# A recurrent layer with its input product in seven half products per chunk of 16 steps

## Chip, cores and metric

The kernel runs on one core of one Trainium2 chip. The metric is the device time of one execution in microseconds. The engines are named as in the profile: PE is TensorE, DVE is VectorE, ACT is ScalarE, POOL is GpSimd, SP is SyncE, which here only issues DMAs.

## What is computed

```python
def reference(x, cond, Wx, Wh, b, W1, b1, W2, b2):     # x: (64, 256, 1024), cond: (64, 1024), all f32
    # layer 0: a recurrence over the 256 steps, and a residual
    xW = einsum('ntd,dh->nth', x, Wx) + b
    h = cond
    for t in range(256):
        h = tanh(h @ Wh + xW[:, t])
        x[:, t] = x[:, t] + h
    # layer 1: a Haar transform along time, every coefficient times one gate, and back, and a residual
    g = silu(cond @ W1.T + b1)
    gate = sigmoid(g @ W2.T + b2)
    return x + haar_back(gate * haar(x))               # = x * (1 + gate) up to rounding, for the gate is one per (n, d)
```

The kernel before and the kernel after both use that the gate doesn't depend on time: each step's x + h is multiplied by a factor made once from the gate. What remains is the recurrence (64 x 1024 by 1024 x 1024, 256 times in sequence) and the product of x with Wx (16384 x 1024 by 1024 x 1024), which depends on nothing but the inputs.

## The kernel before

**The recurrent product.** `h_product` (L208) multiplies the hidden state (64 x 1024, in four quadrants of 32 rows by half the columns) with Wh by seven products of halves (Strassen's scheme in Winograd's form): four sums of quadrants of h are made by DVE in `strassen_sides` (L190), the sums of Wh were made once in `strassen_weight` (L141). Each of the seven is 4 x 4 matmuls of f32 on a quarter of the array's columns (`strassen_product`, L158; the profile shows two matmuls for each). Some results accumulate in the PSUM bank `acc`, into which `put` (L202) has copied the step's row of x Wx beforehand, others in the banks `m16` and `m57`; DVE adds them to y (L222, L225) and h (L229), ACT takes the tanh (L393), DVE transposes h in blocks of 32 x 32 to hT (L395). hT is what the next step's product needs.

**The input product.** `XWork` (L245) does x Wx for a pair of steps, 128 rows at once. DVE splits x into a part of few mantissa bits (`high_bits`, L116), the rest (L253) and a mixture of both (L255), each of them in the reduced f32 form[...]; Wx was split the same way at the start and stays in SBUF. Three products, low, high and mixed, give the full precision. The stationary operand is a block of x (128 x 128), the moving one a half row block of Wx (128 x 512): 8 x 3 x 2 = 48 matmuls of 128x512 for two steps (L237), into the banks `main` and `mixed`. ACT takes `mixed` out (L269), POOL adds the bias (L270), DVE adds `main` (L301). The sum goes to DRAM and comes back as rows for each step (L305, L311).

**The output.** For each step POOL adds hT to x (L416) and multiplies by the factor (L372); SP stores a pair of steps. The first pairs, which are ready ahead of the factor, are kept in DRAM and scaled later.

**What sets the order.** The source gives an order, in which `first` and `second` spread the 48 matmuls of a later pair over two steps, behind the recurrent product of each. The tile framework then plans the order on each engine's queue from expected durations: an instruction that is expected to be ready may go ahead of an earlier one of the source. [...]

## Time and profile before

| | |
|---|---|
| median of 3 runs | 3133.39 us (3131.64 to 3136.84) |
| profiled execution, its own time | 3132.18 us |
| profiled execution, span of the trace | 3130.4 us |
| mean granted clock of PE | 0.997 |
| PE busy | 3090.0 us, 99% |
| DVE busy | 1762.4 us, 56% |
| POOL busy | 1112.9 us, 36% |
| ACT busy | 717.9 us, 23% |
| DMA | 298.54 MB, mean 95 GB/s |

The groups of the page give a mean duration per instruction. For PE it is the time from a matmul's start to its modelled end, and matmuls are pipelined, so the cost of one is read from the timeline as the distance of starts. A duration on DVE or POOL includes the time in which the instruction was held after it had started.

### The profile page before, as it was taken

The numbers are of one execution on the slowest core, as the hardware profiler recorded it, in microseconds if no ns is written. First come the engines' busy times: TensorE is split into PE (matmuls) and PEld (weight loads), VectorE is DVE, ScalarE is ACT, GpSimd is POOL, SyncE is SP. The second block draws the span as 40 slices with busy tenths as digits, with TensorE's granted clock in tenths as the row PEclk, the third lists the DMA queues.
The fourth block names the chain that finished last, engine by engine and source line by source line (L and its number), as shares of the span: only waits on it lengthen the run. The fifth ranks groups of instructions, "written<-read, shape, count | busy, mean of one in ns | idle before, by whom it ended". The sixth has DMA issues, their size and how long they took to land.

```text
span 3130.4 us, 137359 instructions
## 1 busy us (share of the span) xinstructions
PE 3090.0 (99%) x63648; PEld 2696.5 (86%) x63648; DVE 1762.4 (56%) x2736; ACT 717.9 (23%) x1425; POOL 1112.9 (36%) x768
## 2 busy tenths in 40 slices
PE   7999999999999999999999999999999999999998
PEld 4888888888888888888888888888888888888887
DVE  6455555555555555555555555555555555555564
ACT  3222222222222222222222222222222222222221
POOL 0233433333333334333333433333333333333332
PEclk9999999999999999999999999999999999999999
DMA  6332332222222222222222222222222222222222
GB/s 241 114 103 97 103 103 90 93 87 96 89 90 91 89 91 91 92 89 91 92 90 90 92 94 86 93 90 90 91 89 97 85 93 93 90 91 89 91 76 70
DMA packets 146286, 298.54 MB, mean 95 GB/s; under 512 B 25520, under 2 KB 91568, under 8 KB 145712
## 3 DMA queue, kind: packets, MB, share of 16 engines
q1 hardware_dynamic: 142448, 283.99, 26.8%
q8 instruction: 498, 8.16, 1.1%
q10 hardware_dynamic: 3264, 5.77, 0.5%
q14 instruction: 76, 0.62, 0.1%
HBM read 153.88 MB, written 135.79 MB: 93 GB/s over the span
## 4 chain that ended last, share of the span: by engine, by line
PE 97%; DMA 1%; DVE 1%; issue 0%; ACT 0%; SPq 0%; POOL 0%; ACTq 0%; DVEq 0%
PE main L237 30%; PE m L163 29%; PE acc L163 21%; PE mixed L237 16%; DMA w<-w1T 1%; PE gate_ps L180 1%; DMA xw<-sum_d 0%; DVE h L229 0%; DMA h0T<-condT 0%; ACT h L393 0%; DVE hT L395 0%; DVE s L195 0%; DVE s L193 0%; DVE s L194 0%; PE acc L180 0%
## 5 line engine op out<-in xcount | busy, mean ns | idle before, releaser
L416 POOL TENSOR_TENSOR x<-x,hT 128x512 f32<-128x512 f32 x254 | 448.9, 1767 | 1684.2 <-DVE hT L395 1673.3
L237 PE MATMUL main<-wx,x 128*128 128x512 f32 x4096 | 993.0, 394 | 4.9 <-DVE sum L301 2.9
L237 PEld LDWEIGHTS main<-wx,x 128*128 128x128 f32 x4096 | 759.5, 188 | 188.5 <-issue 27.7
L222 DVE TENSOR_TENSOR y<-m,u 128x256 f32<-128x256 f32 x255 | 108.2, 424 | 865.6 <-PE m L163 865.6
L237 PE MATMUL mixed<-wx,x 128*128 128x512 f32 x2048 | 505.6, 398 | 0.0
L163 PE MATMUL m<-t,s 128*32 128x128 f32 x16320 | 494.2, 273 | 2.4 <-DVE s L195 2.4
L237 PEld LDWEIGHTS mixed<-wx,x 128*128 128x128 f32 x2048 | 376.1, 188 | 100.5 <-issue 25.0
L163 PEld LDWEIGHTS m<-t,s 128*32 128x32 f32 x16320 | 452.4, 110 | 3.0 <-issue 2.9
L270 POOL TENSOR_TENSOR sum<-sum,b_row 128x512 f32<-128x512 f32 x256 | 328.8, 1285 | 281.0 <-ACT sum L269 281.0
L393 ACT ACTIVATE h<-h 128x512 f32<-128x512 f32 x256 | 161.9, 633 | 794.7 <-DVE h L229 794.7
L372 POOL TENSOR_TENSOR x<-x,factor 128x512 f32<-128x512 f32 x248 | 336.6, 1358 | 11.5 <-DVE factor L358 1.8
L229 DVE TENSOR_TENSOR h<-acc,y 128x512 f32<-128x512 f32 x255 | 176.4, 692 | 243.5 <-PE acc L163 243.5
L395 DVE STREAM_TRANSPOSE hT<-h 128x512 f32<-128x512 f32 x256 | 182.3, 712 | 204.0 <-ACT h L393 204.0
L163 PEld LDWEIGHTS m<-wh,hT 128*32 128x32 f32 x8160 | 208.1, 109 | 93.1 <-issue 84.9
L255 DVE SCALAR_TENSOR_TENSOR x<-x,x_high 128x1024 fp32r<-128x1024 f32 x128 | 287.7, 2248 | 0.0
L163 PE MATMUL m<-wh,hT 128*32 128x128 f32 x8160 | 276.0, 276 | 4.6 <-DVE hT L395 4.6
L163 PE MATMUL acc<-wh,s 128*32 128x128 f32 x8160 | 272.6, 273 | 2.9 <-issue 2.9
L163 PE MATMUL acc<-t,hT 128*32 128x128 f32 x8160 | 270.5, 273 | 2.1 <-issue 2.1
L163 PE MATMUL acc<-wh,hT 128*32 128x128 f32 x8160 | 271.4, 274 | 1.0 <-ACT acc L205 0.9
L163 PE MATMUL m<-wh,s 128*32 128x128 f32 x8160 | 269.9, 273 | 0.0
L261 ACT CAST x<-x_high 128x1024 fp32r<-128x1024 f32 x128 | 134.0, 1047 | 472.6 <-PE main L237 471.0
L163 PEld LDWEIGHTS acc<-wh,s 128*32 128x32 f32 x8160 | 229.6, 110 | 4.4 <-issue 4.4
(48 smaller groups left out, 2297.5 us busy)
## 6 DMA issues: line engine op xcount, KB each, us to landing
x<-xT SPq DMA_DIRECT2D x128, 512.0 KB, 3.7
sum_d<-sum SPq DMA_DIRECT2D x128, 512.0 KB, 3.0
xw<-sum_d SPq DMA_DIRECT2D x1024, 64.0 KB, 2.0
yT<-x SPq DMA_DIRECT2D x124, 512.0 KB, 3.6
wh<-wh ACTq DMA_DIRECT2D x8, 512.0 KB, 6.6
wx<-wx SPq DMA_DIRECT2D x8, 512.0 KB, 5.8
w<-w1T SPq DMA_DIRECT2D x8, 512.0 KB, 6.9
w<-w2T SPq DMA_DIRECT2D x8, 512.0 KB, 4.0
```

Source lines behind the costliest of these rows:

```text
L163: nc.tensor.matmul(out=out[q * R : (q + 1) * R], lhsT=a[:, k * R : (k + 1) * R], rhs=wh_s[i][k][:, q], start=first and k == 0, stop=k == K ...
L180: nc.tensor.matmul(out=ps[q * R : (q + 1) * R, g * F : (g + 1) * F], lhsT=vT[:, col : col + R], rhs=w[:, q * F : (q + 1) * F], start=k == ...
L222: nc.vector.tensor_add(y[:, 1:3], m57[:, : 2 * E].rearrange("p (i e) -> p i e", i=2), u[:].unsqueeze(1).broadcast_to((P, 2, E)))
L229: nc.vector.tensor_add(h, acc, flat(y))
L237: nc.tensor.matmul(out=acc[h], lhsT=v[:, k * P : (k + 1) * P], rhs=wx_s[k][which][:, h * HALF : (h + 1) * HALF], start=start and k == 0, s ...
L255: nc.vector.scalar_tensor_tensor(out=self.x2, in0=self.x1[:].bitcast(F32), scalar=-UP, in1=self.high, op0=ALU.mult, op1=ALU.add)
L261: nc.scalar.copy(self.x0, self.high)
L270: nc.gpsimd.tensor_add(s, s, b_row[:, h * HALF : (h + 1) * HALF])
L372: nc.gpsimd.tensor_mul(of_step(x, s), of_step(x, s), blocks(factor))
L393: nc.scalar.activation(h, h, AF.Tanh)
L395: nc.vector.transpose(hT, h)
L416: nc.gpsimd.tensor_add(of_step(x, s), of_step(x, s), blocks(hT))
```

## The change

The product of x with Wx is now made for chunks. The first eight steps are two chunks of 4 steps, as are the last eight; between them are 15 chunks of 16 steps.

- **Operands.** Blocks of Wx are stationary, x is the moving operand; the result has the columns of Wx on the partitions, so that the bias is one value for each partition and is added by ACT on its way out.
- **A chunk of 16 steps** is a matrix of two halves of 8 steps (512 rows of x each) by two halves of d; it is multiplied with Wx by seven products of halves in the same scheme as the recurrent product. POOL makes the four sums of x and the sums of results; DVE splits seven operands of two tiles each; where a result is a sum of two products, ACT puts the earlier one into the PSUM bank beforehand.
- **Forms.** The three split forms of the blocks of Wx and of their four sums (seven of the eight are used in a long chunk) are stored in DRAM at the start and in the first four steps, and are streamed to SBUF for each column block, in three buffers of 128 x 1536.
- **Rows.** Results go to DRAM and come back as 64 x 1024 for each step, not yet transposed; `put` is a transpose by DVE from SBUF into the PSUM bank, in place of ACT's copy.
- **Output.** x for the output is loaded for each step apart, in the layout of hT, and stored for each step.
- **Pace.** `due` gives deadlines: five products of a chunk by the step ahead of it, seven by its eighth step; each step of the recurrence does as much x work as the steepest of them asks for.
- The recurrent product has the same matmuls; its quadrants are ordered otherwise.

The core of the diff (removed: `XWork`, `load_x` for pairs, ACT's copy in `put`):

```diff
-        nc.scalar.copy(acc, flat(xw))
+        nc.vector.transpose(acc, flat(v))
...
+    def split_x(x, name: str) -> list:
+        x0 = high_bits(x[:], 2 * HALF, f"high_{name}")
+        out = [split.tile([P, 2 * HALF], F32R, tag=f"x{i}", bufs=(3, 4, 4)[i], name=f"x{i}_{name}") for i in range(3)]
+        nc.vector.tensor_sub(out[1], x, x0)
+        nc.scalar.copy(out[0], x0)
+        nc.vector.scalar_tensor_tensor(
+            out=out[2], in0=out[1][:].bitcast(F32), scalar=-UP, in1=x0, op0=ALU.mult, op1=ALU.add
+        )
+        return out
...
+    def x_banks(name: str) -> list:
+        return [x_pool.tile([P, HALF], F32, tag=tag, name=f"{tag}_{name}") for tag in ("mixed", "main")]
+
+    def take(out, mixed, main, b=0.0) -> None:
+        nc.scalar.activation(out, mixed, AF.Identity if b is not 0.0 else AF.Copy, scale=-DOWN, bias=b)
+        nc.vector.scalar_tensor_tensor(out=out, in0=main, scalar=1.0 + DOWN, in1=out, op0=ALU.mult, op1=ALU.add)
...
+    def load_forms(i: int, j: int, name: str):
+        w = stream.tile([P, KB, FORMS, P], F32R, tag="stream", name=name)
+        nc.sync.dma_start(out=w[:].bitcast(F32).rearrange("p k i f -> p k (i f)"), in_=forms_d[i][j])
+        return w
+
+    def products(banks, w, x, width: int, first: bool, last: bool, onto: bool = False):
+        mixed, main = banks
+        per = 2 * HALF // width
+        for form, out in ((2, mixed), (1, main), (0, main)):
+            for k in range(KB):
+                begins = first and k == 0 and (form == 1 or (form == 2 and not onto))
+                x_matmul(
+                    out, w[:, k, form], x[k // per][form], k % per, form,
+                    begins, last and k == KB - 1 and form != 1, width,
+                )
+            if form or not last:
+                yield width
...
+    def long_chunk(t: int):
...
+        order = ("M1", "M5", "M6", "M3", "M2", "M7", "M4")
+        ready = prepare(order[0])
+        for n, p in enumerate(order):
+            x, i = ready, int(p[1]) - 1
+            base = {"M6": m1, "M3": m5, "M2": m1, "M4": u}.get(p)
+            for j in range(KB):
+                w = load_forms(i, j, f"w{t}_{i}{j}")
+                if j == 0 and n + 1 < len(order):
+                    ready = prepare(order[n + 1])
+                mixed, main = x_banks(f"{t}_{i}{j}")
+                if base:
+                    nc.scalar.activation(mixed, base[j], AF.Copy, scale=-UP)
+                yield from products((mixed, main), w, x, HALF, True, True, onto=base is not None)
...
+                elif p == "M6":
+                    u[j] = part("u", j)
+                    take(u[j], mixed, main)
+                    nc.gpsimd.tensor_add(m5[j], m5[j], u[j])
+                elif p == "M7":
...
+                    take(m7, mixed, main)
+                    nc.gpsimd.tensor_add(results[p][:, :, j], by_rows(m5[j][:]), by_rows(m7[:]))
+                    nc.gpsimd.tensor_add(u[j], u[j], m7)
...
+                if j == KB - 1 and p in ("M3", "M2", "M7", "M4"):
+                    keep_result(results[p], t if p in ("M3", "M2") else half2, BLOCK, int(p in ("M3", "M7")))
+                yield HALF
...
     for t in range(T):
...
+            acc = put(xw_next, t + 1)
+        for _ in range(4):
+            next(weight_sums, None)
+        goal = done + max(((d - done) / max(by - t, 1) for d, by in deadlines if d > done), default=0)
+        while done < goal:
+            done += KB * next(work_x)
+        if t + 1 < T:
+            x_next = load_step(t + 1)
+        if t + 2 < T:
+            xw_next = xw_step(t + 2)
+
+        nc.gpsimd.tensor_add(x, x, hT)
...
+            nc.gpsimd.tensor_mul(x, x, factor)
+            nc.sync.dma_start(out=yT[t], in_=x)
```

## The prediction

> **What bounds the kernel now.** I read first the busy shares, then the chain that ended last, then the groups of its lines.

> ```profile
> PE 3090.0 (99%) x63648; PEld 2696.5 (86%) x63648; DVE 1762.4 (56%) x2736; ACT 717.9 (23%) x1425; POOL 1112.9 (36%) x768
> ...
> PE 97%; DMA 1%; DVE 1%; issue 0%; ACT 0%; SPq 0%; POOL 0%; ACTq 0%; DVEq 0%
> ...
> L237 PE MATMUL main<-wx,x 128*128 128x512 f32 x4096 | 993.0, 394 | 4.9 <-DVE sum L301 2.9
> ...
> L255 DVE SCALAR_TENSOR_TENSOR x<-x,x_high 128x1024 fp32r<-128x1024 f32 x128 | 287.7, 2248 | 0.0
> ```

> PE is busy 99% and is 97% of the chain, so PE work is the time. The timeline of 1505 to 1530 us gives its price: a block of 24 x products (128x512) starts at 1517.38 and the next recurrent product at 1523.04, so one costs 5.66/24 = 0.236 us; a recurrent product takes 6.26 us (1511.12 to 1517.38). A step is 6.26 + 5.66 = 11.92 us. What could replace PE shows in the same timeline, where VectorE and GpSimd hold each other up:

> ```profile
> 1507.80 0.29 DVE L193 TENSOR_TENSOR s<-hT 128x128 f32<-128x128 f32 x1
> 1507.84 1.39 POOL L416 TENSOR_TENSOR x<-x,hT 128x512 f32<-128x512 f32 x1 [8.17 <-DVE hT L395]
> 1508.00 1.38 DVE L194 TENSOR_TENSOR s<-hT 128x128 f32<-128x128 f32 x1
> ...
> 1519.67 1.18 DVE L253 TENSOR_TENSOR x<-x,x_high 128x1024 fp32r<-128x1024 f32 x1
> 1519.82 2.17 POOL L416 TENSOR_TENSOR x<-x,hT 128x512 f32<-128x512 f32 x1 [4.35 <-DVE hT L395]
> ```

> L194 needs 0.29 us but takes 1.38, until the GpSimd add ends; at 1519.82 the add waits for L253 instead. These rows also show the order: L253 of a later pair runs between hT and the sides of this step, so each queue was ordered by a planner that fills expected gaps, not by the source. I therefore do not count every source-order wait as a stall.

> The waits and the stretches give the slack and the DMA rate:

> ```profile
> DVE h L229 <- PE acc L163: 243.5, 255, 2.7
> DVE hT L395 <- ACT h L393: 204.0, 255, 1.2
> ...
> SPq L441 <- POOL x L372: 431.1, 124, 4.8
> ...
> 0.00:40.00 40.00, 26.23 (x228) 11.09 (x231) 28.14 (x34) 13.77 (x13) 0.20 (x4) 1.00 0.88 326
> ...
> 1500.00:2900.00 1400.00, 1400.00 (x29222) 1232.00 (x29215) 788.49 (x1235) 320.25 (x647) 512.78 (x352) 1.00 0.27 91
> ```

> VectorE rests about 0.95 us per step before h and 0.80 before hT (244/255, 204/255). DMA stands at 0.27 in the steady part; at the start it reached 326 GB/s at a share of 0.88. Last, a rest of PE costs more than itself:

> ```profile
> 1511.12 1.08 PE L163 MATMUL m<-wh,hT 128*32 128x128 f32 x32
> ...
> 3104.90 1.33 PE L163 MATMUL m<-wh,hT 128*32 128x128 f32 x32 [2.25 <-DVE hT L395]
> 3105.98 1.95 PE L163 MATMUL acc<-wh,hT 128*32 128x128 f32 x32
> ```

> After 2.25 us of rest the second block of 32 takes 1.95 us where it takes 1.06 in the steady part.

> [...]

> **The change part by part.**

> PE: out go 6144 x products of 512 columns (1450 us). In come 15 chunks of 7 x 4 x 4 x 3 = 336, that is 5040 x 0.236 = 1189 us, and four short chunks of 192 with 256 columns, 768. A 256-column product isn't in the trace: 0.118 (half) if columns set it, 0.188 if the weight load does; I take 0.15, 115 us (91 to 144). **Saved: 146 us (117 to 170)**. A step of a long chunk needs 6.26 + 21 x 0.236 = 11.22 us. The recurrent products keep shape and number.

> VectorE, uncontended, per 16 steps. Kept: h 0.69, hT 0.71, four sides at 0.29, y 0.42 and 0.29. Added: the transpose into PSUM that replaces ScalarE's copy (L205, 0.59). No row shows one into PSUM; below nothing is excluded, since VectorE gets an instruction more; 0.6 to 1.2, and I take hT's 0.71. That is 3.98 a step, 64 in 16 steps. Splits rise from 8 to 14 tiles: 14 x (0.68 + 1.18 + 1.22) = 43; the 1.22 is L126, the same shape without GpSimd beside it, where L255 has 2.25. Evictions rise from 16 to 28 at 0.68: 19. **Sum 126 us per 16 steps, 7.9 a step.**

> GpSimd, per 16 steps: bias adds (16 x 1.285) go, since the bias rides on ScalarE's eviction. Added: eight sums of 128x1024 at about 2.5 (twice L270's 1.285), 20; and twelve of 128x512, 15. The add of hT and the scaling stay, 32 x 1.28 = 41. Sum 76, 4.8 a step, against 4.35 before (1112.9/256).

> Contention: before, the sides cost 2.27 a step (0.843 + 0.825 + 0.310 + 0.289) for 1.16 uncontended, and splits 4.11 a tile for 3.08: 1.6 us a step, 26 per 16, beside 62 us of GpSimd at 1.28, that is 0.54 per GpSimd instruction. VectorE's own two-input and split work grows from 43 to 62 us per 16 steps, so I scale: 0.54 x 62/43 = 0.77, by 60 GpSimd units of 1.28 us, 46 us, **2.9 a step** (1.6 to 3.5). VectorE is then at 10.8 of 11.22 us. The two rests of the chain (0.95, 0.80) come on top unless another instruction fits in: 10.8 if all are filled, 12.5 if none. I take 12.0, **0.8 us a step over PE's need, 190 us in 240 steps** (0 to 305). Queued behind: the transpose into PSUM waits for its DMA, and the takes and splits wait behind it; a take late holds one of two PSUM banks, on which x products wait; a late hT holds the recurrent product.

> ScalarE: tanh 0.63, m copies 0.53, and per 16 steps 28 evictions and 16 preloads of `mixed` at 0.59 and 14 casts at 1.05: 3.7 us a step, hidden under PE; without that cover it would still be a third of the step.

> DMA, per 16 steps: forms 28 x 0.786 = 22.0 MB, x for the chunk 14 x 0.524 = 7.3, results out and in 8.4, x per step and y 8.4: 46 MB in about 180 us, 257 GB/s, a share near 0.7. All are on SP's queue. Three stream buffers give a form's load the time of two column blocks, about 12 us; it needs 0.786 MB/326 GB/s = 2.4 plus some 2 to land (the xw rows' 2.0), and waits behind other transfers. I cost it at nothing in the steady part; the cover is those 12 us, and if SP is held past it each load is late on PE (the second rival).

> Start: until the first recurrent product (74.8 us in the chain) the change moves 13.6 MB of inputs and stores 16 x 0.786 = 12.6 MB of forms, from whose three buffers the products also read: 26.2/326 = 80 us, plus 10 for first landing and the way through DRAM: some 95, **+20**. Until step 7: forms read back 12.6, summed forms stored 12.6, wx again 4.2, the first long chunk 20.9, w2 4.2, the steps' own some 7: 62 MB, 190 us, where PE has 7 x 6.26 + 192 x 0.15 + 240 x 0.236 = 129. If all of that shows, +61; part can be done earlier; I take **+45** (20 to 70). End: x work is done before step 251, so some three more tails of 2.5 us lie open: **+8**.

> Sum on the profiled execution (3132.2 us, span 3130.4, 1.2 below the median of the runs): 3132 - 146 + 65 + 8 + 190 = **3249**, 3250 against the median.

> **The rivals.** *VectorE keeps up* (faster): the planner fills both rests, PE stays the bound. For it: before, VectorE rested 865 us in all before y and 44% in total, and PE lost only 1%. Against: 10.8 of 11.22 leaves 0.4. It decides if VectorE's step stays under 11.22: 3132 - 146 + 65 + 8 = 3059 (3002 to 3110). *Forms come late* (much slower): [...]y's store waits there for GpSimd (431 us in 124 waits already), and loads stand behind it. From a hold of about 5 us (12 less 2.4, 2 and a queued 2 to 3) each load shows. One microsecond over 420 loads (28 x 15) in place of the 190: 3132 - 146 + 73 + 420 = 3479; the slower clock after rests would add to it. *The work isn't saved*: excluded if matmuls fall by 336, 63648 - 6144 + 5808 = 63312, and the long blocks stay at 0.236.

> **How the numbers follow.** 0.2% is about what a measurement here can tell from no change. Forecast 0.55 (3110 to 3390), VectorE keeps up 0.26, late forms 0.17, work not saved 0.02. Of the forecast 0.03 and of the work not saved 0.02 fall within 0.2%; the first rival ends wholly below. Faster 0.26, same 0.05, slower 0.69. The range: from the first rival's best, 3000, to just past the second's value, 3500; under 1 in 10 is left out at each end.

> **What would show it.** Right: PE idle with DVE named as releaser, in the recurrent product's m and in x products after a take; DVE above 85%, sides and splits at or above their means of before; DMA share near 0.7; step 1 some 20 us later. Wrong: PE at 97% or more with steps of 11.2 us (first rival), or PE waiting for DMA of the stream buffers (second). Steps above 13 us with VectorE below 80% would mean that a wait which I cost at nothing sets the time.

## The result, and the profile after

| | before | after |
|---|---|---|
| median of 4 runs | 3133.91 us (3131.64 to 3136.84) | 3379.78 us (3363.59 to 3384.04) |
| profiled execution, its own time | 3132.18 us | 3363.59 us |
| span | 3130.4 us | 3361.8 us |
| mean granted clock of PE | 0.997 | 0.975 |

The kernel became slower: the ratio is 1.0774, with a 95% interval of 1.0738 to 1.0811. That is 246 us by the medians and 231 us between the two profiled executions (that of after was the fastest of its four). Forecast were 117.

The first lines of the profile's page, in the order in which those of before were read: the engines' busy time, the DMA share in 40 slices, two DMA queues, the chain, and the transfers of the forms.

```profile
PE 3035.3 (90%) x63312; PEld 2632.4 (78%) x63312; DVE 2600.4 (77%) x3522; ACT 960.8 (29%) x1744; POOL 1329.8 (40%) x832
...
DMA  9788778786777667676776767677676766766673
...
q1 hardware_dynamic: 342912, 800.71, 70.9%
q8 instruction: 496, 8.13, 1.0%
...
PE 61%; DVE 21%; issue 7%; DMA 6%; POOL 3%; ACT 1%; SPq 1%; ACTq 0%; DVEq 0%; POOLq 0%
...
w<-forms SPq DMA_DIRECT2D x468, 768.0 KB, 5.4
```

The matmuls fell by 336, to the 63312 expected, and yet PE is busy only 90% of a longer span. The chain has gone from 97% PE to 61%, with 21% DVE and, new, 7% "issue": time in which PE waited for nothing that the profile shows. A load of forms lands 5.4 us after its issue, in the median, well inside the 12 us of its buffers.

The same split shows in the waits, over the whole trace (total us, times, longest us):

```profile
DVE h L515 <- PE acc L437: 176.7, 159, 3.2
...
PE m L437 <- DVE hT L583: 97.5, 45, 13.3
...
PE acc L437 <- issue: 61.7, 52, 4.0
...
PE m L437 <- ACT y L502: 22.8, 23, 2.6
PE m L437 <- issue: 22.7, 26, 1.8
...
PE m L437 <- DVE s L475: 18.2, 24, 2.4
```

Before, DVE waited for PE at h in all 255 steps that have a recurrent product; now in 159, and in many of the others PE waits for DVE. The two "issue" lines are 84 us in 78 rests. In the kernel before the counterpart is this, all of it ahead of step 8:

```profile
PE acc L163 <- issue: 4.9, 6, 1.4
```

**Where the time went, by stage.** The matmuls in a stretch of the trace, each at its distance of starts (0.236 us for 512 columns; 0.12 to 0.145 measured for 256, taken as 0.13; 6.26/224 for a recurrent one; 0.066 taken for one of the plain products at the start), give what PE needs there. The rest of the stretch is called lost. All in us; a step's boundary is the end of its hT.

| stage | before: time, need, lost | after: time, need, lost |
|---|---|---|
| to hT of step 0 | 74.8, 42.1, 32.6 | 99.3, 41.9, 57.5 |
| steps 0 to 8 | 105.6, 97.9, 7.7 | 242.3, 148.2, 94.2 |
| 8 to 16 | 97.2, 95.4, 1.8 | 119.6, 95.4, 24.2 |
| 16 to 64 | 574.8, 572.4, 2.5 | 622.2, 571.9, 50.3 |
| 64 to 240 | 2097.1, 2098.6, -1.5 | 2116.5, 1923.7, 192.7 |
| 240 to the end | 180.9, 165.2, 15.7 | 161.9, 129.9, 31.9 |
| sum | 3130, 3072, 59 | 3362, 2911, 451 |

PE's need fell by 161 us. The start lost 111 us more than before, steps 8 to 240 lost 264 more (267 against 3), the end 16: -161 + 111 + 264 + 16 = +230, the measured difference of the spans. Until step 64 the need per step is that of before, since x work runs ahead there with 24 products a step (571.9/48 = 11.9, less 6.26, by 0.236) where the mean is 21.

The 267 us of steps 8 to 240, sorted by the releaser of every rest over 0.3 us (start to start, less the price above): "issue" 107 in 90 rests; hT 63 in 36; ACT's copy L502, which frees the bank m, 28; sides (the sums of quadrants of h) 24; late forms 3; below 0.3 us each 39, slower matmuls after rests among them. After the rest of 5.32 us that ended at 3133.06 us, for one, the first two blocks of 32 took 1.93 us each, where the same blocks at 2082.37 us took 1.08 and 1.06, and the granted clock was 0.50 from 3131.0 to 3137.8 us. In the kernel before, around its block of 1.95 us at 3105.98, it was 0.59 from 3105.0 to 3108.4. The rests for hT, sides and L502 make **115 us**; in e5 below, with GpSimd's output work cut, all three shrink, to 33 together. The granted clock in these steps is 0.99 (0.86 in steps 0 to 8), so what a lower clock costs lies within the 39 and is not the main loss:

```profile
341.70:3199.90 2858.20, 2669.27 (x56842) 2320.70 (x56842) 2311.76 (x3090) 838.31 (x1525) 1218.06 (x755) 0.99 0.71 238
```

The columns are the stretch and its length, busy PE, PEld, DVE, ACT and POOL with their instructions, then PE's clock, the DMA share and GB/s.

How a late hT comes about is in the timeline at 2111.84 us (start, duration, engine and line):

```profile
2111.84 0.69 DVE L131 TENSOR_SCALAR high_A<-A 128x1024 int32<-128x1024 int32 x1
2112.05 1.06 PE L437 MATMUL acc<-wh,s 128*32 128x128 f32 x32
...
2112.56 1.22 DVE L174 TENSOR_TENSOR x_A<-A,high_A 128x1024 fp32r<-128x1024 f32 x1
...
2113.82 1.23 DVE L176 SCALAR_TENSOR_TENSOR x_A<-x_A,high_A 128x1024 fp32r<-128x1024 f32 x1
...
2114.97 0.68 DVE L208 SCALAR_TENSOR_TENSOR resultM<-main,resultM 128x512 f32<-128x512 f32 x1
2115.57 0.41 DVE L508 TENSOR_TENSOR y<-m,u 128x256 f32<-128x256 f32 x1
...
2118.66 1.08 PE L437 MATMUL m<-wh,hT 128*32 128x128 f32 x32 [0.75 <-DVE hT L583]
```

The recurrent product ends at about 2113.0, but DVE's queue has the split of a tile (L131, L174, L176) and a take (L208, which brings an x product out of PSUM) ahead of y. y starts at 2115.57, hT is done at 2118.5, and PE, which has run out of its x products, rests 0.75 us.

An "issue" rest looks otherwise. PE alone, at 2087.63 us:

```profile
2087.63 0.82 PE L437 MATMUL acc<-wh,s 128*32 128x128 f32 x20
2089.47 0.63 PE L437 MATMUL acc<-wh,s 128*32 128x128 f32 x12 [1.01 <-issue]
```

The times of q8's packets in the same trace confirm it. Counted in order, each packet belongs to one block. In steps 8 to 240 all 86 rests end 1.18 to 1.59 us (median 1.39) after the end of the packet for the block that then begins, and PE enters no block, with a rest or without, sooner than 1.18 us after its packet. The packets take no longer than before (median 0.96 us, before 1.05), but they start later: in the median 1.61 us after PE has entered the block ahead (2.61 at the 86 rests), against 0.38 in the kernel before. So PE waits for late instructions; that the DMA load makes them late is what the experiments had to show.

### The profile page after: what moved, and what is told of

The parts are those of the page before. It is cut to its first block, busy times and chain, and to the rows that moved or that the text cites. A ratio compares the mean times of both kernels' runs of the same rounds, so it can differ in the third digit from the quotient of the medians.

```text
span 3361.8 us, 138900 instructions
## 1 busy us (share of the span) xinstructions
PE 3035.3 (90%) x63312; PEld 2632.4 (78%) x63312; DVE 2600.4 (77%) x3522; ACT 960.8 (29%) x1744; POOL 1329.8 (40%) x832
## 3 DMA queue, kind: packets, MB, share of 16 engines
q8 instruction: 496, 8.13, 1.0%
## 4 chain that ended last, share of the span: by engine, by line
PE 61%; DVE 21%; issue 7%; DMA 6%; POOL 3%; ACT 1%; SPq 1%; ACTq 0%; DVEq 0%; POOLq 0%
PE m L437 21%; PE acc L437 16%; PE main L193 15%; PE mixed L193 8%; DMA w<-forms 2%; DVE hT L583 2%; DVE s L475 2%; DVE h L515 2%; DVE high_S L131 2%; DVE acc L491 2%; DVE x_S L176 2%; DVE s L474 1%; DVE x_A L174 1%; DVE s L476 1%; DVE high_A L131 1%
## 5 line engine op out<-in xcount | busy, mean ns | idle before, releaser
L599 POOL TENSOR_TENSOR x<-x,hT 128x512 f32<-128x512 f32 x256 | 357.8, 1398 | 1434.7 <-DVE hT L583 1434.7
L193 PE MATMUL main<-x_S,w 128*128 128x512 f32 x1920 | 491.6, 395 | 2.5 <-DVE resultM L208 1.7
L193 PEld LDWEIGHTS main<-x_S,w 128*128 128x128 f32 x1920 | 356.8, 189 | 91.8 <-issue 16.1
L193 PE MATMUL main<-x_A,w 128*128 128x512 f32 x1440 | 373.0, 399 | 3.0 <-DVE one L208 2.3
L437 PE MATMUL acc<-wh,s 128*32 128x128 f32 x8160 | 295.7, 275 | 37.3 <-issue 36.5
L193 PEld LDWEIGHTS main<-x_A,w 128*128 128x128 f32 x1440 | 270.3, 191 | 70.0 <-issue 11.2
L193 PE MATMUL mixed<-x_S,w 128*128 128x512 f32 x960 | 267.5, 400 | 8.8 <-DMA w<-forms 7.1
L476 DVE TENSOR_TENSOR s<-hT 128x128 f32<-128x128 f32 x255 | 272.1, 1067 | 0.0
L437 PEld LDWEIGHTS acc<-t,hT 128*32 128x32 f32 x8160 | 238.3, 110 | 33.1 <-issue 32.6
L437 PEld LDWEIGHTS m<-wh,s 128*32 128x32 f32 x8160 | 233.9, 110 | 23.8 <-issue 23.5
```

Of the source, the lines that this page charges most:

```text
L193: nc.tensor.matmul(out=out, lhsT=w, rhs=v[:, k * width : (k + 1) * width], start=first, stop=last, skip_group_check=True,)
L437: nc.tensor.matmul(out=out[q * R : (q + 1) * R], lhsT=a[:, k * R : (k + 1) * R], rhs=wh_s[i][k][:, q], start=first and k == 0, stop=k == K ...
L476: nc.vector.tensor_sub(s3, a11, a21)
L599: nc.gpsimd.tensor_add(x, x, hT)
```

## Experiments

Ratios are to the kernel before, measured beside each run (medians 3128 to 3131 us), with 95% intervals. "Lost" and "rests" are counted as above, from the profiled execution of each run.

### Forms kept in SBUF, the output sums cut, and both

**e2_resident**: all products read one block of forms that stays in SBUF, so the values of the input product are others; the forms are still made and stored. To make room in SBUF, the stream has two buffers in place of three.

```diff
+        if not resident:
+            w = const.tile([P, KB, FORMS, P], F32R, tag="resident", name=name)
+            nc.sync.dma_start(out=..., in_=forms_d[i][j])
+            resident.append(w)
+        return resident[0]
```

> The changed kernel with its forms streamed only once: the first block loaded stays in SBUF and every product of x after the first chunk uses it (so those products use the wrong weights); same matmuls, no loads of forms. Theory 1 (instruction fetch behind data): the rests under 'issue', some 105 us in the steady part, go, VectorE's stay: some 3220 us, start shorter by 20 to 60 of it. Theory 2 (VectorE alone): only the start gets shorter, 3310 to 3350. Theory 3 (forms come late in the steady part): nearly all of PE's rest goes, under 3130.

Measured: 3243.39 us, ratio 1.037 (1.0355 to 1.0386), 136 us below after and nearest to the first of the three expectations. Steps 0 to 8 lost 50 instead of 94. In steps 8 to 240 the issue rests fell from 107 to 16 us and the loss from 267 to 196, while the rests for VectorE (hT, sides, the copy) rose from 115 to 141. PE's two largest waits, over the whole trace:

```profile
PE m L440 <- DVE hT L586: 110.3, 59, 13.6
PE m L440 <- ACT y L505: 22.9, 23, 2.6
```

**e5_tiny_output_math**: GpSimd's two output instructions per step on 8 of 512 columns, so most of the output lacks h and the factor; their waits stay. Two causes of VectorE's lateness stand against each other: GpSimd's instructions beside its own, and the place of the long splits in its queue.

```diff
-        nc.gpsimd.tensor_add(x, x, hT)
+        nc.gpsimd.tensor_add(x[:, :8], x[:, :8], hT[:, :8])
...
-            nc.gpsimd.tensor_mul(x, x, factor)
+            nc.gpsimd.tensor_mul(x[:, :8], x[:, :8], factor[:, :8])
```

> The changed kernel with GpSimd's add of hT and its scaling cut to the first 8 of 512 columns (the other columns are stored as loaded), so that loads and stores keep the pace that run e3 lost. [...]PE's rests behind hT, the sides and ACT's copies, 118 us in the steady part of the changed kernel, fall under 50, the 'issue' rests stay near 107: 3260 to 3310 us. If it is the place of the long splits in VectorE's queue: these rests stay above 90, above 3340.

Measured: 3368.93 us, 1.0773 (1.0756 to 1.0789): no gain, for after has 1.0774. Yet the sides fell from 3.17 to 1.51 us a step, here for one of them (busy us, mean ns):

```profile
L476 DVE TENSOR_TENSOR s<-hT 128x128 f32<-128x128 f32 x255 | 99.6, 391 | 0.0
```

In after it is 1067 ns. And PE's waits of e5 (total us, times, longest us) have changed places:

```profile
PE acc L437 <- issue: 124.8, 89, 3.8
...
PE m L437 <- DVE hT L583: 63.9, 26, 11.8
...
PE m L437 <- issue: 39.7, 32, 2.8
```

In steps 8 to 240 the rests for hT, sides and L502 fell from 115 to 33 us, and the issue rests rose from 107 to 197, 126 of 137 at the same place in the 256. GpSimd's contention was real, and without it these rests are 82 us less, but the issue rests, 90 more, took all of it back. So half of what was expected came, the rests under 50, and the time did not. How much of the 82 is the contention itself is not separated: a PE that rests for instructions also gives VectorE time.

**e6_resident_tiny**: both edits. The first outcome is for the case that the fetch and GpSimd's hold on VectorE are all that costs time there.

> The forms of e2 (one block loaded once, so wrong weights) and the cut output math of e5 together. [...]PE's loss from step 8 to 240 falls from 267 to under 80 us and the kernel beats the one before: 3050 to 3120. If a third cause holds PE: above 3150.

Measured: 3147.68 us, 1.0069 (1.005 to 1.0087): 232 us below after, against 136 and 11 for the edits alone, and between the two expected outcomes. In steps 8 to 240: VectorE 52, issue 35, small ones 25, 112 in all. So the loss there falls by 156 us with both edits, by 71 with e2 alone, and rises by 10 with e5 alone. PE's two largest waits:

```profile
PE m L440 <- DVE hT L586: 70.1, 31, 13.3
PE acc L440 <- issue: 32.4, 26, 2.8
```

A step of 64 to 240 takes 11.36 us, less than the 11.92 of before. A rest for VectorE seems to give the fetch time to catch up: with one cause taken away, the rests of the other grew, from 115 to 141 us in e2 and from 107 to 197 in e5. This pair of causes carries 156 of the 267 us; the 112 that stay are open.

### VectorE's amount of work, and the output sums gone

**e4_put_by_scalar**: ScalarE copies the row into `acc`, without the transposition, so the rows enter the recurrence untransposed.

```diff
-        nc.vector.transpose(acc, flat(v))
+        nc.scalar.copy(acc, flat(v))
```

> The changed kernel with ACT's copy in put in place of VectorE's transpose (the rows then enter the step untransposed, so h is another). VectorE loses 0.73 us a step. If VectorE's amount of work sets the steady part: up to 0.73 x 232 = 169 us go, 3210. If it is only where its long splits stand in its queue, or instruction fetch: under 60 us go, above 3320.

Measured: 3359.56 us, 1.0735 (1.0719 to 1.0752), 20 us off the median, though the span, 3358.9, is only 3 below that of after's fastest execution. DVE's busy share in steps 64 to 240 went from 0.81 to 0.76; the loss there stayed (189 for 193). The 0.73 us a step did not set the time, as the second of the expected outcomes has it; the intervals of the two ratios overlap.

**e3_no_output_math**: GpSimd's add of hT and scaling left out altogether, so y is x. Theory 2 of the expectation lays VectorE's lateness to GpSimd's instructions beside its own.

```diff
-        nc.gpsimd.tensor_add(x, x, hT)
...
-            nc.gpsimd.tensor_mul(x, x, factor)
```

> The changed kernel without GpSimd's add of hT and its scaling by the factor (the stored steps are x as loaded; the first eight are still scaled later). GpSimd's work falls by 41 of 76 us per 16 steps, and y's stores no longer wait for it. Theory 2[...]: the sides fall to 0.3 to 0.5 us each, VectorE from 0.81 to under 0.7, and 80 to 130 us go: 3250 to 3300. Theory 1 (instruction fetch): DMA is as before, the 'issue' rests stay, less than 60 us go from contention: above 3320.

Measured: 3450.3 us, 1.1026 (1.101 to 1.1043), slower than after, which no expectation had in mind. Its DMA share in 40 slices says why:

```profile
DMA  9888889999989988855555655556565555654452
```

Without hT in it, the loads and stores of x lost their pace and ran ahead, at a share of 0.8 to 0.9 for the first 17 slices. The sides fell to 1.57 us a step as hoped, but issue rests rose to 178 us and late forms from 3 to 48. As a test of GpSimd's share it failed, and e5 takes its place; as a test of DMA load it speaks for the fetch.

### DMA load added to the kernel before

**e1_before_loads**: two copies per step from DRAM to DRAM, whose data nobody uses.

```diff
+        for n in range(2):
+            d = dram.tile([P, 2, 704], F32, tag="dead", name=f"dead{t}_{n}")
+            nc.sync.dma_start(out=d, in_=wx[...])
```

> The kernel before with two more DMAs per step, 0.72 MB each, from an input to a scratch tensor in DRAM, which nothing waits for; the rest is untouched. Theory 1 (the fetch of PE's instructions shares the DMA engines with the data): DMA share from 0.27 to some 0.65, and PE, which lost nothing before, now rests under 'issue' at one fixed place in each 256 of its instructions; 3200 to 3260 us. Theory 2 (PE's losses after the change come from VectorE alone): data that nobody waits for costs nothing, 3130 to 3145 us.

Measured: 3307.92 us, 1.0579 (1.0553 to 1.0604), above both expectations, with no instruction added on any compute engine. The copies had no pace either. Two stretches, with the columns as above:

```profile
200.00:1700.00 1500.00, 1396.11 (x28097) 1205.84 (x28090) 857.80 (x1192) 311.78 (x621) 507.53 (x344) 0.99 0.84 279
...
2000.00:3000.00 1000.00, 999.74 (x20796) 879.12 (x20792) 564.90 (x882) 228.84 (x461) 367.01 (x252) 1.00 0.27 91
```

At a share of 0.84 PE is idle 104 us of 1500 and a step (20 to 140) takes 13.28 us; back at 0.27 it is 11.92 again. Of the 181 us lost in steps 8 to 240, 109 are issue, 68 of the 82 rests at the 193rd or 194th place; another 42 are rests for ACT's copy into `acc` (L205), which waits for late rows, and 28 are small.

**e11_before_stores2** and **e12_before_stores5**: paced copies instead, hT stored n times in each step.

```diff
+        for n in range(2):          # e12: range(5)
+            nc.sync.dma_start(out=dram.tile([P, W], F32, tag=f"dead{n}", ...), in_=hT)
```

> The kernel before with hT stored twice more in each step (0.52 MB, rows of 2 KB) to scratch tensors that nobody reads; the stores follow the pace of the steps. DMA share from 0.27 to about 0.42. Instruction fetch theory: 0 to 60 us, if rests begin only when the DMA engines are much busier; rival (any more traffic is harmless, e1 was slow for its rows arriving late): within 10 us of before.

> As e11 with five such stores in each step (1.3 MB): DMA share near 0.65 over the whole span. Instruction fetch theory: 'issue' rests at the same place of each 256 instructions, 100 to 250 us, 3230 to 3400. Rival: within 30 us of before, with rests for rows only.

Measured: 3137.25 us, 1.0021 (1.0011 to 1.003), and 3173.82 us, 1.0138 (1.0123 to 1.0153). e12 is 43 us slower, between the two outcomes expected of it: past the rival's 30, and well short of what the fetch theory forecast. The stretch of 500 to 2500 us in e11:

```profile
500.00:2500.00 2000.00, 1999.82 (x41655) 1758.84 (x41654) 1128.66 (x1763) 458.57 (x924) 733.12 (x503) 1.00 0.39 135
```

and in e12:

```profile
500.00:2500.00 2000.00, 1991.21 (x41172) 1743.94 (x41171) 1120.88 (x1743) 454.78 (x916) 727.35 (x499) 1.00 0.56 199
```

In the one kernel, the issue rests of steps 8 to 240 thus go with the DMA share: 0.27 none, 0.39 0.4 us, 0.56 18.8 us (32 rests, all at the 193rd or 194th place), 0.84 109 us in about half of the span. After, at 0.71, has 107. The load makes them, though in e12 they are only part of its 48 us: 16 more are rests for late rows (L205) and 13 are small. The fetch itself follows the load: its packets start, in the median, 0.38 us after PE has entered the block ahead in before and e11, 0.81 in e12 and 1.05 in e1, while a packet takes about 1 us in all of them. What holds the start, the trace doesn't say.

The share alone doesn't fix the size of the rests: e2 and e6 stand at 0.40 and have 16 and 35 us. Their packets start later than those of e11 too, at 0.60 and 0.70 us.

### The start

**e7_no_weight_sums**: the sums of blocks of Wx are neither formed, stored nor read in the first steps; long chunks use other forms in their place, so their values are others.

```diff
-        for _ in range(4):
-            next(weight_sums, None)
...
-                w = load_forms(i, j, f"w{t}_{i}{j}")
+                w = load_forms((0, 1, 2, 0, 1, 2, 0)[i], j, f"w{t}_{i}{j}")
```

> The changed kernel without the four sums of Wx and their forms (the products that need them use three others, so the result is wrong; the traffic of the stream is the same). 12.6 MB of stores and 4.2 MB of loads fall away in the first steps, and GpSimd's and VectorE's work for them. If the amount of data sets the start: hT of step 8 comes 45 to 65 us earlier than at 342, the kernel ends near 3320. If the start waits for single transfers in turn: under 20 us.

Measured: 3303.68 us, 1.0565 (1.0539 to 1.0591). Steps 0 to 8 took 177.6 us instead of 242.3 and lost 29 instead of 94; PE's rests for forms there fell from 40 to 4 us. Making the sums, with the loads of Wx for it, and storing them costs the start 65 us; the stream reads as much as before.

### Two attempts at the causes

**e8_interleaved**: from step 8 on, two groups of four of the step's x products among the seven recurrent products, so that no 256 PE instructions in a row are recurrent.

```diff
         strassen_product(c11, a[2], B21)
+        some_x()
...
         strassen_product(m16, a[6], T2)
+        some_x()
```

> The changed kernel from step 8 on with two groups of four x products between the recurrent products (after the second and after the fourth of the seven), the rest behind them as before; same work, the whole result. PE's instructions come at a more even rate. If PE outruns the fetch only in the dense recurrent products: the 'issue' rests fall from 107 to under 60 us and the kernel to 3300 to 3340. If the rests follow the DMA load alone: they stay near 107, and less cover behind the recurrent product makes it slower, 3370 to 3430.

Measured: 3519.59 us, 1.1257 (1.124 to 1.1273), outside both expectations. The issue rests fell from 107 to 21 us, as they should if PE outruns the fetch only in a dense run of recurrent matmuls. But an x product inside the recurrent one is missing behind it, where it covered VectorE's tail:

```profile
PE m L437 <- DVE hT L591: 189.4, 89, 12.8
```

In steps 8 to 240 that is 162 us where after has 63, and the small losses rose from 39 to 189; why they do where the two kinds of matmul alternate, the trace doesn't say.

**e9_short_rows**: each load of forms as four, with shorter rows.

```diff
-        nc.sync.dma_start(out=w[:]..., in_=forms_d[i][j])
+        for k in range(KB):
+            nc.sync.dma_start(out=w[:, k]..., in_=forms_d[i][j, :, k])
```

> The changed kernel with each load of forms made as four DMAs with rows of 1.5 KB in place of one with rows of 6 KB; same bytes, same work, the whole result. If a fetch of instructions waits for the long rows ahead of it on each DMA engine, the 'issue' rests fall from 107 to under 60 us: 3300 to 3340. If only the amount of data counts: 90 to 140 us of such rests, 3360 to 3420.

Measured: 3359.02 us, 1.0734 (1.0715 to 1.0753), whose interval overlaps that of after. Issue rests fell from 107 to 69 us, late forms rose from 3 to 16 and the rests for VectorE from 115 to 124. The issue rests came near what was expected of long rows in the way of the fetch (under 60), the time did not (3300 to 3340). No gain is resolved.

### What the saved products are worth alone

**e10_seven_of_eight**: the kernel before with one of the eight blocks of d left out of x Wx from the second pair on.

```diff
-            for k in range(B):
+            for k in range(B - 1):
```

> The kernel before with 42 of its 48 products of x per pair from the second pair on (one block of eight of the contraction is left out, so xW is incomplete): PE's saving of the change alone, with no other part of it. 127 x 6 x 0.236 = 180 us. If the saving comes through when nothing else changes: 2945 to 2965. If the shorter cover behind the recurrent product (4.96 us in place of 5.66) shows: above 2990.

Measured: 2982.89 us, 0.9527 (0.9512 to 0.9542): 148 us less, for 127 x 6 x 0.236 = 180 us of products, between the two expected outcomes. Its step is 11.34 us, near the 11.2 that after's PE needs, with the DMA and splits of the kernel before. In steps 8 to 240 it lost 37 us, of which 15 are rests for late rows (L205) and 6 are issue rests, where before lost 3. So most of such a saving comes through when nothing else is added; in after it was lost to what was added for it. It isn't a kernel to use, for it computes less.

## Where the prediction was right and where wrong

Between the profiled executions the forecast was +117 us, the spans give +230. By terms, measured against forecast: PE -161 against -146, the start +111 against +65, the end +16 against +8, the steady part (steps 8 to 240) +264 against +190. That the kernel became slower was forecast. That the error is only 113 us is in part luck: VectorE's term was too large, which hid much of one that was put at nothing.

**PE's saving: right.** 161 us by counts against 146 (117 to 170). The 0.188 of a weight load was read here, on the page of before:

```profile
L237 PEld LDWEIGHTS main<-wx,x 128*128 128x128 f32 x4096 | 759.5, 188 | 188.5 <-issue 27.7
```

For the 256-column products a load takes 194 ns in the mean (`main<-x,w`, L193), and yet their starts are 0.12 to 0.145 us apart, where I took 0.15: the load doesn't bound them.

**VectorE: right in kind, the term was too large.** The mean step of 8 to 240 is 12.32 us against my 12.0, with 1.15 us lost (267/232) against 0.8, and less than half of that, 115 of 267, stands in rests for VectorE. The parts: transpose into PSUM 0.73 us against 0.71, contention some 2.6 us a step (sides 3.17 less 1.16; splits 3.79 a tile less 3.08, by 14/16) against 2.9. The takes out of PSUM, to which I gave no contention, showed none: 0.675 us in the mean (L208), 0.677 in the kernel before (L301). Of the signs, PE's rests for DVE ahead of m and longer sides came. VectorE above 85% did not (0.81 in steps 64 to 240), nor splits at their mean of before (3.79 us a tile, before 4.11), nor rests in x products after a take (none over 0.3 us in steps 8 to 240). The forecast 190 us are 115 us of rests, plus part of the 39 small. And e4 shows that I counted the wrong thing: the sum of VectorE's time didn't decide. How long GpSimd holds it counts (e5: 33 us of rests in place of 115). That what stands in its queue ahead of y and hT counts too is read from the timeline; no run tests it.

**The step that failed: "I cost it at nothing in the steady part".** The share I forecast for DMA, 0.7 (257 GB/s, by the start's 326 at 0.88), came (0.71), and the cover I named, 12 us of stream buffers, held: late forms cost 3 us. What was missing is a second customer of the DMA, the fetch of PE's instructions ("q8 instruction", 8.13 MB). e1, e11 and e12 show that DMA load alone makes PE rest (109, 0.4 and 18.8 us); the place in each 256, the packet size and the packets' times show that it waits for instructions. That is 107 us in after, where the term had 0. 115 + 107 + 39 + 3 = 264 of the 267 us lost, where I had 190. In the kernel before, at a share of 0.27, these steps have no such rest.

**The start: right in kind, mis-sized.** To the first hT +25 against +20; steps 0 to 8 +87 against +45. The 62 MB were nearly right (242.4 us at 284 GB/s are 69 MB):

```profile
99.30:341.70 242.40, 170.94 (x2386) 141.16 (x2387) 145.70 (x201) 69.56 (x115) 64.56 (x39) 0.86 0.81 284
```

I took 326 GB/s, the peak of before's first 40 us, for all of it, and supposed that part of the excess could be done earlier. With 284 the same 62 MB take 218 us, 89 over the 129 that I had for PE. The summed forms cost 65 us (e7), the stream 44 (e2); together that is more than the 94 lost, so the two overlap. **The end**: +16 against +8.

**The rivals.** That VectorE keeps up was wrong. That forms come late was near the truth in suspecting DMA and wrong in the mechanism for the steady part: loads landed in 5.4 us, and PE waited 3 us for them. In steps 0 to 8, which this rival did not speak of, forms did come late: PE rested 40 us for them, once for 19.9 us. Its waits from 99 to 342 us have this line:

```profile
PE mixed L193 <- DMA w<-forms: 37.3, 12, 19.9
```

That the work isn't saved is excluded by 63312 matmuls. The sign for "a wait which I cost at nothing" that I named, steps above 13 us, was set too coarse: the wait was there at 12.32.

**Open.** What remains in e6 (112 us); what holds the start of the fetch, and so why equal shares of DMA (e2 and e11) give different issue rests; the small losses of e8; and whether a kernel that computes the whole result can have the saving without the stream. The runs show no version that beats before.

## What to carry to other kernels

When a change trades PE work for streamed data, cost the DMA share itself, not only whether the loads land in time: look in the trace for "issue" rests at a fixed place in every 256 PE instructions, the sequencer's own counted. Here, at a share of 0.71, 86 of 90 stood at one place, and 83 lay inside the recurrent products with their 0.028 us a matmul. Take away suspected causes in pairs as well as singly: here the loss of steps 8 to 240 changed by -71 and +10 us apart and by -156 together. And give an added copy a pace (data of the same step), or it may run ahead and test something else, as e1 did at a share of 0.84 and e3 at 0.8 to 0.9.

## What the runs showed of the hardware

I had not expected that the fetch of instructions could be late at all. With the data queues at a share of 0.71, PE stood still for it for 107 us in 232 steps, 86 times of 90 at the same place in a block of 256, and stores of hT alone, at 0.56, made 18.8 us of it in the kernel before. After each of the 86 rests PE went on 1.18 to 1.59 us after the 16 KB packet of its next block had ended. Added load made these packets start later, not take longer: 0.38 us after the start of the block ahead in the kernel before, 0.81 in e12 and 1.05 in e1 (1.61 in after), at about 1 us for a packet in all (median 1.05 in before, 0.96 in after). Whether the data queues hold them on the DMA engines or elsewhere is not shown. Next to it, a StreamTranspose of 128x512 f32 from SBUF into PSUM takes 726 ns in the mean, beside 705 for hT in SBUF.
